# A two-layer graph kernel on one core: row sums of the neighbour lists on four column strips of TensorE, and two ScalarE steps in another order

## The chip, the core and the metric

One core of a Trainium2 chip runs the whole kernel. The metric is the device time of one execution in microseconds (us). Before the change three runs gave 2482.44, 2485.44 and 2485.81 us, so the median is 2485.44 us.

The engines are TensorE (PE; its weight loads are shown as PEld), VectorE (DVE), ScalarE (ACT), GpSimd (POOL) and SyncE (SP, which here only issues DMAs). Each works through its own queue in order, and they meet at semaphores.

## The reference

The input is a batch of 16 graphs with 1024 nodes and 64 features each, and an adjacency matrix of integers per graph, in which about 0.8% of the entries are set. Two layers follow each other, each with a residual and a layer norm:

```python
x = _layernorm(x + _L0_gnn_ref(x, adj, ...))   # eight heads
x = _layernorm(x + _L1_gnn_ref(x, adj, ...))   # one head
```

Layer 0 is attention in eight heads of 64 over the neighbours, with a bias per kind of edge and a leaky ReLU before the softmax:

```python
scores = einsum('bmhd,bnhd->bhmn', q, k) * scale + edge_bias
scores = leaky_relu(scores, 0.2); masked where edges == 0
out = einsum('bhmn,bnhd->bmhd', softmax(scores), v) @ Wp + bp
```

Layer 1 scores a pair by a leaky ReLU of a sum of two projections, weighed by a vector `a`:

```python
s = u[:, :, None, :] + v[:, None, :, :]
e = einsum('bijf,f->bij', where(s > 0, s, 0.2 * s), a); masked where adj == 0
h_prime = softmax(e) @ hp; return elu(h_prime)
```

## The kernel before, in words

Since few entries of the adjacency are set, the kernel works on lists of neighbours. Rows come in groups of eight (`GR`); a tile `t` holds 128 rows as 64 rows on each half of the partitions, and a batch has eight tiles (`NT`).

**The lists.** `prepare(b)` (from L318) is a generator that builds the lists of graph `b` in small pieces. For each half of the columns (`hs`) it loads eight tiles of the adjacency, turns each into bf16 zeros and ones in `ab` (L335), clears the diagonal on POOL (L340), and then adds up, for each group of eight rows and each column, a code in which every row of the group has its own bit. That is the sum over rows `pat` (L346): a matmul of `wz`, which holds the codes, with each of the eight `ab` tiles, 512 columns at a time. The 16 groups of tile `T` belong in the rows `16 T` to `16 T + 15` of `pat`. `wz` is mostly zero, and a window of 128 of its columns puts the block of codes where tile `T` needs it; all eight matmuls write all 128 rows of one PSUM bank and accumulate. DVE then reads `pat` into keys `ka` (L351) and picks the largest with max and match-replace (L357 to L392). At the end SP writes the lists to memory, from where they return as `cb`, spread over all partitions.

**One iteration.** The loop over `g` at the end of the kernel handles tile `g` of layer 0 and tile `u = g - 12` of layer 1. `at(layers, step, name)` issues one step of one tile, and the order of these calls is the order of each engine's queue: it was written out by hand, and nothing reorders it. `lists.place(g, k)` issues, at five places of an iteration, the pieces of list work that are due, and pieces of norm work. `t` is `g` modulo eight; some work comes only at certain `t`: the end of layer 1 of a graph at `t = 6`, the constants of the next graph at `t = 7`, the start of layer 1 at `t = 2` and its `sums` at `t = 3`.

The steps that matter here, in the order of an iteration:

- `score` (L642 on PE), which DVE reads into `sc` (L650); `gather` of layer 0 (L516 on PE, copied to `xg` on ACT, L522); `heads` (L710, odd tiles); `rows` into `back` (L289, L726); `queries` (L621, read on DVE into `qp`, L626).
- `residual` of both layers on DVE (L843, L732), which reads `back`.
- `project` of layer 1 (L777, L783): ACT and then DVE read `pz` into `r` (L789, L790).
- `gather` of layer 1, first half; then `turn_weights` of layer 1 (one transpose on PE, L818, and the copy `eT` on ACT, L820); then `turn` of layer 0 (eight transposes on PE, L535, and two copies `xn` on ACT, L536); then `gather` of layer 1, second half.
- `weigh` of layer 1 (L804 on PE: 12 matmuls in four strips of 32 columns into the bank `e`; DVE takes the row maximum `m`, L806), then `exps` of layer 1 (the exponential on ACT, L812, which needs `m`).
- `turn_weights` of layer 0 (L684 on PE into `pp`, two copies `w` on ACT, L686); `turn` of layer 1 (L535, L536).
- `own_rows` (the copy `rw` on ACT, L767, then `rq` on POOL, L769); `attend` of layer 0 (L694 on PE into `z`, which needs `w`; copied to `zT` on ACT, L699); `attend` of layer 1 (L829 on PE into `pa`, copied to `aT` on ACT, L834).

**Shared PSUM.** `back`, the transposed `eT` and the scores of `weigh` follow each other in one buffer (tag `e`): each must be read before the next is written. `z` and `pat` share another single buffer (tag `z`). The transposes `pt` of layer 0, `pp` and `pq` share two buffers (tag `p`), `pg`, `pa` and the transposes of layer 1 two more (tag `g`), and the scores `s`, `po` and `pz` two of tag `s`.

Of the kernel before, what the change touches and what calls it, by code (L numbers as in the profile page):

```python
# [12 lines left out]
ALU = mybir.AluOpType  # L13
# [16 lines left out]
BF16 = mybir.dt.bfloat16  # L30
# [3 lines left out]
def kernel(  # L34
# [4 lines left out]
    nc = tc.nc  # L39
    B, N, D = x.shape  # L40
    H = edge_bias.shape[1]
    HD = H * D
    P = 128
    NT = N // P
# [8 lines left out]
    fst = fast.enter_context(tc.tile_pool(name="fst", bufs=1))  # L53
# [15 lines left out]
    def sub(n):  # L69
        return slice(n * D, n * D + D)  # L70
# [42 lines left out]
    for h in range(H):  # L113
        c, r = h // 2, sub(h % 2)
# [89 lines left out]
    NGT = P // GR  # L204
# [10 lines left out]
    code_w = tmp.tile([P, 1], F32, name="code_w")  # L215
# [6 lines left out]
    in_g = fst.tile([P, NGT], F32, name="in_g")  # L222
# [4 lines left out]
    nc.vector.tensor_tensor(in_g, in_g, lt_g, ALU.mult)  # L227
    in_q = fst.tile([P, NQ], F32, name="in_q")
    nc.vector.tensor_tensor(in_q, in_g[:, 0:NQ], in_g[:, NQ : 2 * NQ], ALU.add)
    wz = fst.tile([P, 2 * P - NGT], BF16, name="wz")  # L230
    nc.vector.memset(wz, 0.0)
    nc.vector.tensor_scalar(wz[:, P - NGT : P], in_g, code_w, None, ALU.mult)
    rep_q = fst.tile([P, NQ, H, GR], BF16, name="rep_q")
    nc.vector.tensor_tensor(
        rep_q, in_q.unsqueeze(2).unsqueeze(3).to_broadcast([P, NQ, H, GR]),
# [82 lines left out]
    def prepare(b):  # L318
# [10 lines left out]
        for hs in range(2):  # L329
            ab = per.tile([P, NT, 2, SEG], BF16, tag="ab", name=f"ab_{b}_{hs}")  # L330
            for T in range(NT):
                ad = ads.pop(hs * NT + T)

                if b:
                    nc.vector.tensor_scalar(ab[:, T, :, :], ad, 1.0 - TINY, 0.0, ALU.subtract, ALU.max)  # L335
                else:
                    nc.scalar.activation(ab[:, T, :, :], ad, AF.Relu, bias=below)
                if T % 4 // 2 == hs:
                    own = ab[:, T, T // 4, ts(T % 2, P)]
                    nc.gpsimd.tensor_tensor(own, own, no_diag, ALU.mult)  # L340
                load(hs * NT + T + 4)
                if T % 2:
                    yield "sums" if T == NT - 1 else None
            pat = ps_z.tile([P, 2, SEG], F32, tag="z", name=f"pat_{b}_{hs}")
            for T in range(NT):
                nc.tensor.matmul(  # L346
                    pat.rearrange("p a c -> p (a c)"), wz[:, P - NGT - NGT * T : 2 * P - NGT - NGT * T],
                    ab[:, T, :, :].rearrange("p n (t r) -> p t n r", r=D), start=(T == 0), stop=(T == NT - 1),
                )
            yield "keys"  # L350
            nc.vector.scalar_tensor_tensor(  # L351
                ka[:, 2 * hs : 2 * hs + 2, 0:SEG], pat, float(KEY), revc.unsqueeze(1).to_broadcast([P, 2, SEG]),
                ALU.mult, ALU.add,
            )
            yield
            for s in range(2 * hs, 2 * hs + 2):
                nc.vector.max(lst[:, s, 0:8], ka[:, s, 0:SEG])  # L357
                nc.vector.match_replace(kb[:, s, 0:SEG], lst[:, s, 0:8], ka[:, s, 0:SEG], -1.0)
                yield
# [66 lines left out]
        for n in range(2):  # L426
            for q in range(NQ):
                r = slice(D * n + GR * q, D * n + GR * q + GR)
# [7 lines left out]
    def finish(b):  # L436

        flags, dg, rows_s = late.pop(b)
        mask = dbl.tile([P, NT, SLOTS], BF16, tag="mask", bufs=3, name=f"mask_{b}")
        nc.vector.tensor_scalar(mask[:, :, 0 : 2 * CAP2], rows_s, code, NEG, ALU.not_equal, ALU.mult)  # L440
        yield
        dgf = sml.tile([P, NT], F32, tag="dgf", bufs=2, name=f"dgf_{b}")
        nc.vector.tensor_scalar(dgf, dg, 1.0, None, ALU.is_ge)
        own = sml.tile([P, NT, GR], F32, tag="own", bufs=2, name=f"own_{b}")
        nc.vector.tensor_tensor(
            own, dgf.unsqueeze(2).to_broadcast([P, NT, GR]), own_i.unsqueeze(1).to_broadcast([P, NT, GR]), ALU.mult
        )
        nc.vector.tensor_scalar(mask[:, :, 2 * CAP2 : SLOTS], own, 0.0, NEG, ALU.is_equal, ALU.mult)
        yield
        nc.vector.tensor_scalar(dgf, dg, 2.0, None, ALU.is_ge)  # L450
        nc.vector.tensor_reduce(flags[:, 18:19], dgf, XX, ALU.max)
        fl = sml.tile([P, 1], F32, tag="fl", bufs=2, name=f"fl_{b}")
        nc.vector.tensor_reduce(fl, flags, XX, ALU.max)
        nc.vector.tensor_scalar(fl, fl, 0.5, None, ALU.is_ge)
        nc.vector.tensor_tensor(bad, bad, fl, ALU.max)
        masks[b] = mask
# [17 lines left out]
    class Tiles:  # L474


        def load(self, t):
            nm = f"{self.b}_{self.layer}_{t}"
            self.cb[t] = cb = dbl.tile([P, NSEG, 2, NQ, WIN], BF16, tag="cb", bufs=3, name=f"cb_{nm}")
            nc.sync.dma_start(  # L480
                cb.rearrange("p s n q k -> p (s n q k)"),
                edges[self.b][t].rearrange("s n q k -> (s n q k)").unsqueeze(0).to_broadcast([P, NSEG * 2 * NQ * WIN]),
            )
# [390 lines left out]
    l0, l1 = {}, {}  # L874

    def at(layers, step, name, *args):
        b, t = divmod(step, NT)
        if b in layers:
            getattr(layers[b], name)(t, *args)
# [28 lines left out]
    lists = Lists()  # L908
    with tc.manual_schedule(engines={getattr(mybir.EngineType, e) for e in order}):
        first = prepare(0)  # L910
        for _ in range(PIECES - 1):
            next(first)
        l0[0] = Layer0(0)
        for _ in lists.side.pop():
            pass
        l0[0].load(0)
        l0[0].load(1)
        l0[0].constants()
        for _ in first:
            pass  # L920
        l0[0].indicate(0)
        l0[0].own(0)
        for _ in finish(0):
            pass
        for g in range(NT * B + LAG + 7):
            u = g - LAG
            b, t = divmod(g, NT)
            if t == 0 and 0 < b < B:
                lists.side.insert(0, finish(b))
            lists.place(g, 0)  # L930
            at(l0, g - 2, "exps", 0, range(4))
            at(l0, g - 1, "score", lambda: at(l0, g - 2, "divide", 0))
            if (g - 1) // NT not in l0:
                at(l0, g - 2, "divide", 0)
            back = ps_z.tile([P, 3, D], F32, tag="e", name=f"back_{g}") if g > 3 else None
            at(l0, g - 2, "exps", 1, range(2))
            at(l0, g, "gather", 0)
            at(l0, g - 3, "heads")
            at(l0, g, "gather", 1)
            at(l0, g - 2, "exps", 1, range(2, 4))  # L940
            at(l1, u - 3, "rows", back)
            at(l0, g - 3, "rows", back)
            at(l0, g, "queries")
            if t == 6 and b - 2 in l1:
                lists.side.append(l1[b - 2].end())
            at(l1, u - 3, "residual")
            at(l0, g - 3, "residual")
            at(l0, g - 2, "divide", 1)
            at(l1, u - 1, "project")
            lists.place(g, 1)  # L950
            at(l1, u, "gather", 0)
            at(l1, u - 2, "turn_weights")
            at(l0, g - 1, "turn")
            lists.place(g, 2)
            at(l0, g + 1, "indicate")
            at(l0, g + 2, "load")
            at(l1, u, "gather", 1)
            at(l1, u - 1, "weigh")
            at(l1, u - 1, "exps")
            if t == 2 and b - 1 in l0:  # L960
                x1 = l0[b - 1].end()
            at(l0, g - 2, "turn_weights")
            at(l1, u - 1, "turn")
            lists.place(g, 3)
            at(l1, u + 1, "indicate")
            at(l1, u + 2, "load")
            at(l0, g + 1, "own")
            at(l1, u + 1, "own")
            at(l1, u, "own_rows")
            if t == NT - 1 and b + 1 < B:  # L970
                l0[b + 1].constants()
            at(l0, g - 2, "attend")
            at(l1, u - 2, "attend")
            lists.place(g, 4)
            if t == 2 and b - 1 in l0:
                l1[b - 1] = Layer1(b - 1, x1)
                del l0[b - 1]
                l1[b - 1].load(0)
            if t == 3 and b - 1 in l1:
                l1[b - 1].sums()  # L980
            if t == 4 and b + 1 < B:
                l0[b + 1] = Layer0(b + 1)
            if t == NT - AHEAD and b + 1 < B:
                l0[b + 1].load(0)
# [415 lines left out]
```

## Time and profile before

The profile is of one execution. Its own time was 2491.47 us, of which 2489.6 us are the span from the first to the last instruction.

| what | value |
|---|---|
| time of the profiled execution | 2491.47 us |
| its span | 2489.6 us |
| mean granted clock of TensorE | 0.969 |
| `pat` matmuls (L346), count and mean duration | 256, 390 ns |
| DVE keys `ka` waiting for `pat` | 114.2 us in 31 waits |
| layer 1's exponential (L812), count and mean duration | 128, 362 ns |
| copies `w` (L686), count and mean duration | 256, 588 ns |
| copies `xn` (L536), count and mean duration | 512, 601 ns |
| copies `eT` (L820), count and mean duration | 128, 269 ns |

A row of the groups' table gives the line, the engine, the operation and the tiles, then the busy time and the mean duration of one. Matmuls overlap, so the busy time of a group of them is less than count times duration. A line of the list of waits reads: engine, its tile and line, what it waited for, then the total in us, the number of waits and the longest. A wait is put down to the last releaser that the profile can see, which is not always the real one. In a timeline each line gives the start and the length in us, and in brackets the time for which the engine sat idle before it and who ended that.

Idle time of an engine which is not the one that sets the pace costs nothing; what a wait is worth must be read from the stretch in which it stands.

### The profile page before, as it was taken

To read this page: it belongs to the slowest core of one execution; us is meant where nothing else is said; L and a number is where in the kernel's file an instruction comes from. 1 tells how busy PE (TensorE), PEld (TensorE's weight loads), DVE (VectorE), ACT (ScalarE), POOL (GpSimd) and SP (SyncE) were. 2 spreads that over 40 slices of the span, in tenths; PEclk is the share of its full clock that TensorE was granted. 3 is DMA by queue.
4 is the path that set the end of the run, shared out by engine and by line. 5 is a ranking of instruction groups with operands and counts; after the bars stand their busy time and mean duration, and the time that the engine had idled before them with its cause. 6 is when DMAs were issued, how large, how long until landed. Compare 5 with 4: busy or idle time off the path is not lost. (4 is left out here: it accounts for less than half of the span.)

```text
span 2489.6 us, 107460 instructions
## 1 busy us (share of the span) xinstructions
PE 2260.9 (91%) x46658; PEld 1870.6 (75%) x46658; DVE 1813.8 (73%) x4591; ACT 1613.4 (65%) x5585; POOL 1206.3 (48%) x1570
## 2 busy tenths in 40 slices
PE   5577999999999999999999999999999999999995
PEld 3466878787787877778787777878777787888764
DVE  5688788687877868687787868778786877866432
ACT  2255666667676676766666676766766676677853
POOL 1133535545454554545455454545545454545552
PEclk8798999999999999999999999999999999999998
DMA  4422422423333242333324232332433233132111
GB/s 103 131 70 93 132 90 76 145 78 108 107 95 109 71 144 85 104 94 101 104 85 135 87 113 83 112 103 79 142 90 110 82 113 103 57 104 71 61 38 29
DMA packets 192691, 238.78 MB, mean 96 GB/s; under 512 B 91732, under 2 KB 157332, under 8 KB 192212
## 3 DMA queue, kind: packets, MB, share of 16 engines
q1 hardware_dynamic: 192212, 231.85, 30.1%
q8 instruction: 368, 6.03, 1.0%
q14 instruction: 111, 0.91, 0.1%
HBM read 226.58 MB, written 5.21 MB: 93 GB/s over the span
## 5 line engine op out<-in xcount | busy, mean ns | idle before, releaser
L516 PE MATMUL pg<-f,x 128*64 128x272 bf16 (+2 forms) x13312 | 811.7, 274 | 44.0 <-DVE f L492 29.0
L516 PEld LDWEIGHTS <-x 128*64 128x64 bf16 x13312 | 669.5, 110 | 154.0 <-issue 125.2
L676 POOL TENSOR_TENSOR ls<-ls,den 128x480 f32<-128x480 f32 x256 | 295.0, 1152 | 641.2 <-DVE den L675 640.1
L522 ACT COPY xg<-pg 128x448 f32<-128x448 f32 x512 | 268.0, 526 | 338.7 <-PE pg L516 338.1
L492 DVE TENSOR_SCALAR f<-cb,jrow 128x2176 bf16<-128x2176 bf16 x512 | 432.4, 885 | 15.0 <-DMA cb<-col_d 15.0
L668 ACT ACTIVATE ls<-ls,mx 128x120 f32<-128x120 f32 x1024 | 390.9, 385 | 0.0
L536 ACT COPY xn<-pt 120x512 f32<-120x512 f32 x512 | 277.9, 601 | 21.7 <-PE pt L535 21.6
L535 PE MATMUL pt<-ident,xg 128*120 128x128 f32 x2048 | 272.6, 275 | 19.6 <-DVE qp L626 17.2
L769 POOL TENSOR_TENSOR rq<-rw,in_q 128x960 bf16<-128x960 bf16 x128 | 229.9, 1796 | 114.8 <-ACT rw L767 114.8
L535 PEld LDWEIGHTS pt<-ident,xg 128*120 128x120 f32 x2048 | 230.7, 138 | 27.9 <-DVE qp L626 18.7
L650 DVE TENSOR_TENSOR sc<-s,rowc 128x480 f32<-128x480 f32 x256 | 156.0, 651 | 120.8 <-PE s L642 119.0
L694 PE MATMUL z<-w,xn 120*64 120x64 f32 x4096 | 173.2, 227 | 65.9 <-ACT w L686 65.8
L694 PEld LDWEIGHTS z<-w,xn 120*64 120x64 f32 x4096 | 146.6, 138 | 99.4 <-ACT w L686 93.9
L789 ACT ACTIVATE r<-pz 128x480 f32<-128x480 f32 x256 | 131.8, 567 | 123.1 <-PE pz L783 123.1
L790 DVE SCALAR_TENSOR_TENSOR r<-pz,r 128x480 f32<-128x480 f32 x256 | 155.6, 649 | 72.6 <-ACT r L789 72.3
L668 ACT ACTIVATION_READ_ACCUMULATOR ls<-ls,mx 128x1 f32 x1024 | 194.4, 190 | 0.0
L658 DVE SCALAR_TENSOR_TENSOR ls<-sc 128x480 f32<-128x480 f32 x256 | 181.3, 708 | 0.0
L659 DVE TENSOR_REDUCE mx<-ls 128x4 f32<-128x480 f32 x256 | 167.2, 653 | 8.8
L501 POOL COPY xg<-xT 128x64 f32<-128x64 f32 x256 | 104.0, 421 | 111.8 <-PE pt L535 111.8
L626 DVE TENSOR_TENSOR qp<-pq,qb 128x256 f32<-128x256 f32 x256 | 96.2, 417 | 76.8 <-PE pq L621 76.8
L642 PE MATMUL s<-xg,qp 64*64 64x120 f32 x4096 | 148.0, 286 | 4.1 <-DVE qp L626 3.4
L829 PE MATMUL pa<-eT,xn 120*64 120x8 f32 x4096 | 145.7, 202 | 4.8 <-ACT xn L536 3.9
(228 smaller groups left out, 4181.0 us busy)
## 6 DMA issues: line engine op xcount, KB each, us to landing
cb<-col_d SPq DMA_DIRECT2D x271, 544.0 KB
ad<-in_adj_dram SPq DMA_DIRECT2D x256, 256.0 KB
xs<-in_x_dram SPq DMA_DIRECT2D x32, 128.0 KB
rows_s<-slot_d SPq DMA_DIRECT2D x256, 14.0 KB
out_dram<-o SPq DMA_DIRECT2D x32, 128.0 KB
col_d<-col SPq DMA_DIRECT2D x128, 4.2 KB
dg<-in_adj_dram SPq DMA_DIRECT2D x32, 2.0 KB
slot_d<-slot SPq DMA_DIRECT2D x16, 28.0 KB
```

What stands on the lines that cost most here:

```text
L492: nc.vector.tensor_scalar(fj.rearrange("p s n q k -> p (s n q k)"), cb.rearrange("p s n q k -> p (s n q k)"), jrow[:, j : j + 1], None, AL ...
L516: nc.tensor.matmul(pg[sub(n), :, FIRST * a_ + lo : FIRST * a_ + to], self.t3[:, k, 4 * hs + 2 * a_ + j, :], f[j][:, 2 * hs + a_, n, :, lo:to],
L522: nc.scalar.copy(dst, pg)
L535: nc.tensor.transpose(pt[:, q, :], xg[:, 4 * m + q, :], ident)
L536: nc.scalar.copy(self.xn[t][:, ts(m, 4), :], pt)
L650: nc.vector.tensor_tensor(sc, both[n], self.rowc[:, n, ts_].unsqueeze(2).to_broadcast([P, 4, SLOTS]), ALU.add)
L658: nc.vector.scalar_tensor_tensor(ls, scs[n], SLOPE, scs[n], ALU.mult, ALU.max)
L659: nc.vector.tensor_reduce(self.mx[:, n, ts_], ls, XX, ALU.max, negate=True)
L668: nc.scalar.activation(ls[:, q, :], ls[:, q, :], AF.Exp, bias=neg[:, q : q + 1], accum_out=den[:, q : q + 1])
L676: nc.gpsimd.tensor_tensor(ls, ls, den.unsqueeze(2).to_broadcast([P, 4, SLOTS]), ALU.mult)
L694: nc.tensor.matmul(zz[sub(n), q, :], xn[:, q, sub(n)], w_[n][:, q // 2, sub(q % 2)], start=True, stop=True)
L769: nc.gpsimd.tensor_tensor(rq, rw.unsqueeze(1).to_broadcast([P, NQ, SLOTS]), in_q.unsqueeze(2).to_broadcast([P, NQ, SLOTS]), ALU.mult)
```

## The change

Three edits.

1. `wz` shrinks from 240 columns to 48: 16 zero columns, the 16 columns of codes, 16 zero columns.
2. The eight `pat` matmuls no longer write all 128 rows. Each writes 32 rows with a window of 32 columns of `wz`: tiles 0 and 1 write rows 0 to 31, tiles 2 and 3 rows 32 to 63, and so on. The even tiles come first and start their strip, then the odd tiles add to it and end it.
3. In an iteration, `turn` of layer 0 now stands before `turn_weights` of layer 1, and `exps` of layer 1 stands behind `turn_weights` of layer 0 and `turn` of layer 1. As these calls set the queues, the transposes L535 come before L818 on PE and the copies `xn` before `eT` on ACT; and the exponential L812 comes behind the copies `w` and `xn` on ACT. Nothing else moves: `weigh` and the maximum `m` stay, and so does every call to `lists.place`.

```diff
-    wz = fst.tile([P, 2 * P - NGT], BF16, name="wz")
+    wz = fst.tile([P, 3 * NGT], BF16, name="wz")
     nc.vector.memset(wz, 0.0)
-    nc.vector.tensor_scalar(wz[:, P - NGT : P], in_g, code_w, None, ALU.mult)
+    nc.vector.tensor_scalar(wz[:, NGT : 2 * NGT], in_g, code_w, None, ALU.mult)
...
-            for T in range(NT):
+
+            for T in (*range(0, NT, 2), *range(1, NT, 2)):
                 nc.tensor.matmul(
-                    pat.rearrange("p a c -> p (a c)"), wz[:, P - NGT - NGT * T : 2 * P - NGT - NGT * T],
-                    ab[:, T, :, :].rearrange("p n (t r) -> p t n r", r=D), start=(T == 0), stop=(T == NT - 1),
+                    pat[16 * (T - T % 2) : 16 * (T - T % 2) + 32, :, :].rearrange("p a c -> p (a c)"),
+                    wz[:, NGT - NGT * (T % 2) : NGT - NGT * (T % 2) + 32],
+                    ab[:, T, :, :].rearrange("p n (t r) -> p t n r", r=D), start=(T % 2 == 0), stop=(T % 2 == 1),
                 )
...
             at(l1, u, "gather", 0)
+            at(l0, g - 1, "turn")
             at(l1, u - 2, "turn_weights")
-            at(l0, g - 1, "turn")
             lists.place(g, 2)
             at(l0, g + 1, "indicate")
             at(l0, g + 2, "load")
             at(l1, u, "gather", 1)
             at(l1, u - 1, "weigh")
-            at(l1, u - 1, "exps")
             if t == 2 and b - 1 in l0:
                 x1 = l0[b - 1].end()
             at(l0, g - 2, "turn_weights")
             at(l1, u - 1, "turn")
+            at(l1, u - 1, "exps")
             lists.place(g, 3)
```

## The prediction

> **What bounds the kernel now.** First the page's busy shares, then busy time by stretches. I cut the steady part at the first score matmul of layer 1 (`weigh`, L804), one stretch for each of eight iterations, and name a stretch by the `t` of the iteration whose `weigh` opens it. The columns are stretch, length, busy PE, PEld, DVE, ACT, POOL, granted clock, DMA share, GB/s. In order they are t = 6, 7, 0, 1, 2, 3, 4, 5.
>
> ```profile
> PE 2260.9 (91%) x46658; PEld 1870.6 (75%) x46658; DVE 1813.8 (73%) x4591; ACT 1613.4 (65%) x5585; POOL 1206.3 (48%) x1570
> 1018.54:1036.76 18.22, 15.51 (x320) 13.01 (x318) 11.34 (x26) 13.82 (x52) 12.49 (x18) 1.00 0.49 160
> 1036.76:1057.27 20.51, 19.70 (x432) 15.53 (x430) 13.10 (x35) 14.29 (x58) 9.70 (x16) 1.00 0.38 135
> 1057.27:1075.51 18.24, 16.89 (x320) 14.19 (x318) 14.73 (x35) 11.60 (x41) 11.59 (x17) 0.91 0.46 136
> 1075.51:1093.88 18.37, 18.37 (x368) 14.62 (x366) 11.83 (x35) 12.57 (x44) 5.06 (x7) 1.00 0.18 63
> 1093.88:1112.12 18.24, 16.29 (x351) 13.77 (x349) 17.48 (x52) 11.46 (x35) 7.92 (x11) 1.00 0.18 65
> 1112.12:1132.67 20.55, 19.20 (x392) 16.33 (x390) 16.93 (x41) 12.56 (x44) 10.14 (x13) 0.92 0.44 121
> 1132.67:1149.62 16.95, 16.95 (x383) 14.69 (x381) 14.32 (x31) 11.93 (x36) 12.37 (x14) 1.00 0.19 69
> 1149.62:1166.07 16.45, 16.45 (x359) 13.83 (x358) 12.73 (x34) 11.60 (x40) 6.79 (x9) 1.00 0.23 49
> ```
>
> The reader sees that PE never rests in t = 1, 4 and 5: there, a microsecond off PE is a microsecond off the time. PE idles in t = 6, 0, 2, 3. In t = 2 DVE is busy 17.48 of 18.24: what PE gains there DVE may take back. In t = 0 and 3 the mean clock is below 1. Next the list of waits, for what PE idles on.
>
> ```profile
> PE z L694 <- ACT w L686: 65.8, 123, 1.5
> ACT e L812 <- DVE m L806: 112.3, 100, 2.4
> PE pt L818 <- DVE den L675: 19.5, 26, 1.2
> ```
>
> The first two belong together, as the timeline of t = 2 shows (start, length, engine, line):
>
> ```profile
> 1095.40 1.04 PE L535 MATMUL pt<-ident,xg 128*120 128x128 f32 x8
> 1096.63 0.27 DVE L806 TENSOR_REDUCE m<-e 128x1 f32<-128x120 f32 x1
> 1096.94 0.36 ACT L812 ACTIVATE e<-e,m 128x120 f32<-128x120 f32 x1 [2.42 <-DVE m L806]
> 1097.29 1.06 ACT L686 COPY w<-pp 120x512 f32<-120x512 f32 x2
> 1097.92 0.33 PE L694 MATMUL z<-w,xn 120*64 120x64 f32 x2 [1.48 <-ACT w L686]
> ```
>
> The maximum `m` is late because DVE has list work first. ACT waits 2.42 us for it with the copies `w` queued behind the exponential, and PE waits 1.48 us for `w`, whose inputs were there all along. By stretch, over the eleven batches of eight stretches from 579 to 2187 us, the z wait is 0.33 us in t = 6, 1.35 in t = 0, 1.64 in t = 2, 1.25 in t = 3, none elsewhere. Its companion is the clock:
>
> ```profile
> 1065.00:1067.00 2.00, 2.00 (x37) 1.58 (x28) 1.36 (x5) 1.20 (x7) 2.00 (x4) 0.50 0.81 234
> ```
>
> Read in 1 us stretches, the clock falls to half for some 3.4 us 13 times in these batches, each costing 1.7 us: five in t = 0, one in t = 2, seven in t = 3, all 5 to 6 us after `weigh`, just behind a z wait; never in the other stretches.
>
> Last, the sums and what speaks for four strips:
>
> ```profile
> 933.82 1.90 PE L346 MATMUL pat<-ab,wz 128*128 128x512 bf16 x8
> 935.64 1.05 PE L642 MATMUL s<-xg,qp 64*64 64x120 f32 x32
> ...
> 1002.15 0.62 PE L804 MATMUL e<-r,a_two 128*32 128x120 f32 x16
> 1002.59 0.24 PE L804 MATMUL e<-mask,ident_b 128*32 128x120 bf16 x4
> ...
> 1018.22 0.27 ACT L820 COPY eT<-pt 120x128 f32<-120x128 f32 x1
> 1018.54 0.36 PEld L804 LDWEIGHTS e<-r,a_two 128*32 128x32 f32 x16 [0.24 <-ACT eT L820]
> ```
>
> Eight sums take 1.82 us to the next group; at 379 ns each and 1.90 in all they start 0.217 us apart, one after another. `weigh` already uses four strips of 32 columns: its four bf16 matmuls of 216 ns each all lie within 0.24 us. The last two lines are t = 6, where `weigh` waits for the copy `eT`.
>
> [...] no run shows four strips at 512. [...] Here a 128x32 bf16 load takes 97 ns against 98 for the 128x128, so I charge nothing for it. [...]
>
> **The change part by part.** All sums are against the profiled execution, 2491.47 us (span 2489.6 and 1.9 around it); the median of the runs is 2485.44, so I subtract 6.0 at the end.
>
> *Sums.* Four strips side by side, two rounds: 2 x 0.217 = 0.43[...] (the bf16 group of `weigh` needs 0.17 to the next start with one short round), 0.59 against 1.82: 1.23 saved. Of 32 groups 26 lie from 310 us on, in t = 7 and 1: 32 us. The six before wait for POOL, ACT and DVE (9.4, 2.2 and 2.0 us in all); I take 2 us. What is late next in t = 1 is `zT`, whose release the sums need (same PSUM ring). Without the exponential in front, ACT must wait for the first transposes `pp`, some 0.3 us more than now, so `zT` ends 0.15 us too late there: 13 x 0.15 = -2. DVE idles 3 to 4 us before it reads the sums, so it follows. Sum: 32. Bounds: 0 if the strips run in turn, 41 if all 32 groups gain 1.27. The setup edit (a smaller `wz`) is one memset behind the weight preparation: nothing.
>
> *Late exponential.* `w` now follows `pp` directly, and z can start when L535 ends. The exponential then waits for `m` behind the copies `xn`, about 3.4 us after `weigh`; `m` comes at 3.0 at worst, and its result is needed only in the next iteration. Behind it on ACT are `rw` (for POOL) and `zT`, needed late except for the sums. For t = 0 I followed the stretch from 1788 us: with PE 1.2 us earlier the DVE times stay, but `pz` still finds `sc`, the transposes find `qp` and `weigh` finds `r` (margins 0.5, 0.2 and 0.9 us). All 1.35 us count: 13 batches, 17.6. In t = 2 they do not: `sc` ends at 1105.64, fixed by DVE, and `pz` starts at 1106.08, so only 0.4 is gained. In t = 3 the u sum on DVE comes earlier by its own wait of 1.25 us, then `po` waits for `sc`; I find `po` near 1121.25 instead of about 1122.2 (1123.57 less one clock drop), so 0.95 for t = 2 and 3 together: 12.4. Sum 30; bounds 8 (DVE takes all but t = 0 in part) and 58 (no DVE limit).
>
> *Clock.* 13 drops in 11 batches, 26 us over 13 batches. If z no longer waits they have no cause; but new waits of 1.1 us or so appear before `pz`, `po` and, in t = 6, `weigh`. The waits of 1.17 and 1.20 us in t = 6 beside gathers never brought a drop. I take half, 13; bounds -10 and 26.
>
> *Order of the turns.* L535 goes before L818, and so two `xn` copies (1.09 us) before `eT` on ACT. Gain: L818 waits for DVE's read of `back` (same PSUM ring), 1.18 us in t = 6 and 0.29 in t = 2; now L535 fills that. Loss: `weigh` needs `eT` gone. In seven stretches the second `xn` copy ends 0.77 us before `weigh`, so `eT` behind it leaves about 0.6. In t = 6 it ends 0.93 after: `weigh` starts 1.0 late, and everything behind it (`pp`, z, `m`), while POOL's norm chain, which sets the middle of that stretch, shifts by about 0.2. So I let t = 6 lose 0.2 net: -3; bounds -24 (the full 1.0 and a clock drop every second time) and +6.
>
> The sum: 32 + 30 + 13 - 3 = 72. 2491.5 - 72 = 2419.5; as a median 2413.5, rounded to 2413.
>
> **The rivals.**
> - DVE takes the place of the z wait: nothing from the exponential in t = 2 and 3, half in t = 0, and the clock no better: 32 + 9 - 3 = 38, 2447. For: 17.48 of 18.24. Against: t = 0 and 3 hold DVE waits for PE.
> - DVE does not bind and all drops go: 32 + 58 + 26 + 6 = 122, 2363. Against: `sc` in t = 2.
> - The strips run in turn, so that the change doesn't do what it says: 0 + 30 + 13 - 3 = 40, 2445. Against: `weigh`.
> - Slower: `eT`, last of three ACT copies, gates `weigh` in every stretch, not in one of eight. My margin is 0.6 us; if the copy comes later than that by 0.56 us in each of 128 stretches, the 72 us are gone, and from there it decides. At 0.7 us, 90 us lost: 2503. Against: ACT idles 0.26 to 0.88 us before the next copy `xg` in those stretches.
>
> **How the numbers follow.** Forecast 0.56; DVE 0.17; everything 0.14; strips in turn 0.05; slower 0.08. The forecast's own range is 2398 to 2430. The range of 8 in 10 takes in the two cases at 2445 and 2447 and half of the third: 2378 to 2450. A change of under 0.2% (5 us) can't be told from none. Faster 0.89, same 0.03, slower 0.08.
>
> **What would show it.** L346: eight matmuls in about 0.6 us. L694 without waits for `w`; L812 without stalling `w`. No half clock behind z in t = 0 and 3. New: PE waiting before L777 in t = 2 and L710 in t = 3, `weigh` waiting for `eT` in t = 6. L804 waiting for `eT` everywhere, or drops in t = 6, would make it wrong.

## The result, and the profile after

The changed kernel takes 2476.05 us (median of 20 runs, 2469.09 to 2485.86), the kernel before on the same chip 2487.56 us (20 runs, 2479.69 to 2500.03). The ratio is 0.9948, 95% interval 0.9936 to 0.9959: about 0.5% faster, some 12 us where 72 were forecast, and outside the forecast's range. The profiled execution has a span of 2474.2 us and a mean clock of 0.964, below the 0.969 of before.

First the page's busy shares, then the same eight stretches as before (t = 6, 7, 0, 1, 2, 3, 4, 5, cut at `weigh`; length, busy PE, PEld, DVE, ACT, POOL, granted clock, DMA share, GB/s):

```profile
PE 2230.1 (90%) x46658; PEld 1852.8 (75%) x46658; DVE 1858.2 (75%) x4591; ACT 1602.8 (65%) x5585; POOL 1227.3 (50%) x1570
```

```profile
1007.87:1024.33 16.46, 15.32 (x317) 12.86 (x318) 12.09 (x25) 12.66 (x50) 11.50 (x16) 1.00 0.52 173
1024.33:1044.80 20.47, 18.34 (x432) 14.87 (x430) 14.10 (x36) 14.25 (x58) 10.56 (x17) 1.00 0.39 136
1044.80:1060.40 15.60, 15.60 (x319) 13.04 (x317) 14.37 (x34) 11.56 (x42) 10.29 (x15) 1.00 0.51 158
1060.40:1077.54 17.14, 17.14 (x367) 14.04 (x365) 13.11 (x36) 12.49 (x44) 6.73 (x9) 1.00 0.22 68
1077.54:1095.21 17.67, 16.66 (x351) 14.04 (x350) 16.95 (x50) 11.28 (x35) 7.34 (x10) 1.00 0.19 67
1095.21:1117.31 22.10, 19.12 (x392) 15.88 (x390) 18.93 (x44) 12.50 (x44) 11.77 (x14) 0.92 0.39 112
1117.31:1134.11 16.80, 16.80 (x384) 14.59 (x382) 14.33 (x31) 11.85 (x36) 12.37 (x14) 1.00 0.19 70
1134.11:1151.38 17.27, 16.35 (x360) 13.72 (x358) 12.71 (x34) 12.50 (x43) 6.95 (x9) 1.00 0.19 48
```

Two things stand out. The instruction counts are the same, yet DVE is busy 44 us longer (1858.2 against 1813.8). And t = 0 and 1 are shorter with PE at work throughout, while t = 3 is longer than before (22.10 against 20.55), with DVE busy 18.93 us instead of 16.93. The means over the eleven steady batches say the same, in us, with some of the kernels tried below:

| stretch | 6 | 7 | 0 | 1 | 2 | 3 | 4 | 5 | sum |
|---|---|---|---|---|---|---|---|---|---|
| before | 18.21 | 20.16 | 17.71 | 18.36 | 18.37 | 19.94 | 16.96 | 16.44 | 146.15 |
| after | 16.46 | 21.13 | 15.65 | 17.14 | 17.67 | 22.77 | 16.80 | 17.26 | 144.88 |
| `strips_only` | 18.22 | 20.75 | 16.79 | 17.12 | 19.07 | 19.04 | 16.94 | 16.43 | 144.36 |
| `rq_late` | 16.46 | 21.43 | 15.66 | 17.11 | 17.79 | 19.76 | 16.80 | 17.26 | 142.27 |
| `rqlate_const5` | 16.46 | 19.66 | 15.70 | 17.11 | 17.79 | 19.47 | 16.80 | 18.48 | 141.47 |
| `best_quota` | 16.53 | 18.22 | 16.41 | 17.08 | 17.54 | 18.43 | 16.80 | 18.38 | 139.39 |

From before to after, t = 6, 0, 1 and 2 gain 1.75, 2.06, 1.22 and 0.70 us a batch; t = 3 gives back 2.83, t = 7 0.97 and t = 5 0.82. (The wait for `eT` ahead of t = 6's `weigh` is counted in t = 5.)

The list of waits shows what PE idles on now:

```profile
PE po L712 <- DVE sc L652: 45.3, 14, 4.7
PE pz L779 <- DVE sc L652: 13.9, 15, 1.0
PE e L806 <- ACT eT L822: 13.2, 15, 0.9
PE z L696 <- ACT w L688: 5.6, 16, 1.2
```

The wait of z for `w` is gone as forecast, 65.8 down to 5.6. The wait of `po` for `sc` was 6.8 us in all and is 45.3: most of what the exponential gave has turned into it. It stands in t = 3. Here is the timeline of that stretch (start, length, engine, line; in brackets the idle time before, and who ended it):

```profile
1099.03 0.38 ACT L769 ACTIVATE rw<-mask,ones 128x120 bf16<-128x120 bf16 x1
1099.47 3.01 DVE L494 TENSOR_SCALAR f<-cb,jrow 128x2176 bf16<-128x2176 bf16 x2
1099.49 2.40 POOL L771 TENSOR_TENSOR rq<-rw,in_q 128x960 bf16<-128x960 bf16 x1 [0.77 <-ACT rw L769]
...
1105.71 1.21 DVE L652 TENSOR_TENSOR sc<-s,rowc 128x480 f32<-128x480 f32 x2
1106.41 1.06 PE L712 MATMUL po<-zT,wvp 64*64 64x128 f32 x6 [2.98 <-DVE sc L652]
```

And the same place before:

```profile
1115.69 1.47 DVE L492 TENSOR_SCALAR f<-cb,jrow 128x2176 bf16<-128x2176 bf16 x2
1117.15 0.43 ACT L767 ACTIVATE rw<-mask,ones 128x120 bf16<-128x120 bf16 x1
1117.66 1.79 POOL L769 TENSOR_TENSOR rq<-rw,in_q 128x960 bf16<-128x960 bf16 x1 [2.67 <-ACT rw L767]
```

Before, `rw` came after the pair of `f`, since ACT had stood waiting 2.13 us for the maximum `m`, with the exponential, `w`, `xn` and `rw` following each other in its queue (they start at 1114.90, 1115.25, 1116.19 and 1117.15). Freed of that wait, ACT issues `rw` before the pair, and POOL's `rq` starts 0.02 us behind DVE's first `f`. Now both take longer: the pair 3.01 us instead of 1.47, `rq` 2.40 instead of 1.79. The maxima and `sc` behind the pair in DVE's queue are late by as much, and PE waits 2.98 us for `sc`. The view in 2 us stretches shows the price behind the wait (the seventh value is the clock):

```profile
1104.00:1106.00 2.00, 0.00 (x0) 0.00 (x0) 1.97 (x6) 0.01 (x1) 0.61 (x1) 1.00 0.67 197
1106.00:1108.00 2.00, 1.59 (x22) 1.31 (x26) 1.97 (x5) 0.00 (x0) 0.91 (x1) 0.56 0.89 264
1108.00:1110.00 2.00, 2.00 (x32) 1.53 (x26) 1.56 (x3) 0.63 (x2) 0.40 (x1) 0.59 0.80 276
```

PE does nothing from 1104 to 1106, and its clock halves just after. In the eleven batches this comes in every t = 3; PE time lost to the half clock there is 2.17 us a batch (1.09 before), while the 0.78 us of t = 0 are gone.

The sums themselves did what the edit says, as the timeline of t = 7 shows:

```profile
1031.11 0.62 PE L347 MATMUL pat<-ab,wz 128*32 128x512 bf16 x8
1031.65 0.82 PEld L644 LDWEIGHTS s<-xg,qp 64*64 64x64 f32 x32 [0.42 <-issue]
...
1032.84 1.35 PE L518 MATMUL pg<-f,x 128*64 128x272 bf16 x22
1035.35 0.42 PE L518 MATMUL pg<-f,x 128*64 128x272 bf16 x4 [1.15 <-issue]
```

Eight matmuls now take 0.54 us to the start of the next group, against 1.82. But some 2.5 us into what follows PE stops for 1.15 us in the middle of a run of equal matmuls with no releaser in the profile ("issue"). Such waits come to 0.32 us a batch in t = 7 before and 1.45 after. Together with a wait of 0.98 us for the copy `xg` (0.20 before) they eat the gain there.

### The profile page after: what moved, and what is told of

Read it like the earlier page. It is cut to its first block, busy times and chain, and to the rows that moved or that the text cites. A ratio compares the mean times of both kernels' runs of the same rounds, so it can differ in the third digit from the quotient of the medians.

```text
span 2474.2 us, 107346 instructions
## 1 busy us (share of the span) xinstructions
PE 2230.1 (90%) x46658; PEld 1852.8 (75%) x46658; DVE 1858.2 (75%) x4591; ACT 1602.8 (65%) x5585; POOL 1227.3 (50%) x1570
## 5 line engine op out<-in xcount | busy, mean ns | idle before, releaser
L518 PE MATMUL pg<-f,x 128*64 128x272 bf16 (+2 forms) x13312 | 822.5, 276 | 43.5 <-DVE f L494 28.7
L494 DVE TENSOR_SCALAR f<-cb,jrow 128x2176 bf16<-128x2176 bf16 x512 | 457.9, 935 | 11.4 <-DMA cb<-col_d 11.4
L537 PEld LDWEIGHTS pt<-ident,xg 128*120 128x120 f32 x2048 | 224.2, 138 | 66.3 <-DVE qp L628 33.5
L771 POOL TENSOR_TENSOR rq<-rw,in_q 128x960 bf16<-128x960 bf16 x128 | 235.8, 1842 | 69.7 <-ACT rw L769 69.6
L688 ACT COPY w<-pp 120x512 f32<-120x512 f32 x256 | 138.1, 590 | 63.2 <-PE pp L686 63.2
L696 PE MATMUL z<-w,xn 120*64 120x64 f32 x4096 | 155.4, 229 | 5.6 <-ACT w L688 5.6
L503 POOL COPY xg<-xT 128x64 f32<-128x64 f32 x256 | 110.9, 450 | 93.1 <-PE pt L537 93.0
L696 PEld LDWEIGHTS z<-w,xn 120*64 120x64 f32 x4096 | 135.9, 141 | 28.2 <-ACT w L688 27.5
L779 PE MATMUL pz<-xg,w2d 64*64 64x480 f32 x1024 | 143.0, 571 | 13.9 <-DVE sc L652 13.9
```

Source lines behind the costliest of these rows:

```text
L494: nc.vector.tensor_scalar(fj.rearrange("p s n q k -> p (s n q k)"), cb.rearrange("p s n q k -> p (s n q k)"), jrow[:, j : j + 1], None, AL ...
L518: nc.tensor.matmul(pg[sub(n), :, FIRST * a_ + lo : FIRST * a_ + to], self.t3[:, k, 4 * hs + 2 * a_ + j, :], f[j][:, 2 * hs + a_, n, :, lo:to],
L537: nc.tensor.transpose(pt[:, q, :], xg[:, 4 * m + q, :], ident)
L696: nc.tensor.matmul(zz[sub(n), q, :], xn[:, q, sub(n)], w_[n][:, q // 2, sub(q % 2)], start=True, stop=True)
L771: nc.gpsimd.tensor_tensor(rq, rw.unsqueeze(1).to_broadcast([P, NQ, SLOTS]), in_q.unsqueeze(2).to_broadcast([P, NQ, SLOTS]), ALU.mult)
L779: nc.tensor.matmul(pz[n][sub(c_), :, :], w2d[sub(n), :], xg[sub(n), :, :].rearrange("p (g c) k -> p c g k", c=2)[:, c_, :, :], start=True, ...
```

## The experiments

The theory was that POOL's `rq`, moved into DVE's `f`, sets t = 3. The rivals were that one of the two order edits is bad by itself, that the sums don't pay, and that DVE has too much list work in t = 2 and 3 whatever POOL does. In the diffs, lines are against the kernel named.

**The parts of the change alone.** `strips_only` undoes both order edits in the changed kernel, `order_only` makes them alone in the kernel before.

```diff
-            at(l0, g - 1, "turn")
             at(l1, u - 2, "turn_weights")
+            at(l0, g - 1, "turn")
...
             at(l1, u - 1, "weigh")
+            at(l1, u - 1, "exps")
...
             at(l1, u - 1, "turn")
-            at(l1, u - 1, "exps")
```

> Only the sums on four strips; both order edits are undone. Theory A (the order edits cost in the stretch t = 3 what they gain elsewhere: POOL's rq now runs at the same time as DVE's f, f's busy time there rises from 5.1 to 7.0 us and po waits 3 us for sc): the strips alone keep their 1.28 us in each of the 26 groups of the steady part, about 30 us, ratio to before near 0.988, and PE shows no wait before po in t = 3. Theory B (the strips' gain itself is lost in t = 7 and 1, to ACT and POOL): ratio 0.993 to 0.997.

Measured: 2463.47 us, ratio 0.9913 (0.9884 to 0.9942). The sums alone give 22 us, more than the whole change, though less than the 0.988 that was expected of them. They gain 1.24 us a batch in t = 1; in t = 7 they lose 0.59, with 1.68 us of waits without a releaser. In t = 3 of the eleven batches PE has no wait for `sc`.

For `order_only` the same lines, the other way round, in the kernel before.

> Only the two order edits, sums as before. Theory A: slower than before by about 16 us, ratio 1.006, with the same wait of some 3 us before po in t = 3 and a half clock there in every batch. Theory B: the order edits gain some 10 us by themselves, ratio 0.996 or less.

Measured: 2488.77 us, ratio 1.0011 (0.9999 to 1.0023): nothing that can be told from no change, and so between the two expectations. Its stretches explain how: t = 6 and 0 win 1.74 and 1.96 us a batch, and t = 3 loses 2.45. The half clock comes in nine of the eleven t = 3, not in every one.

```profile
PE po L710 <- DVE sc L650: 43.4, 14, 4.7
```

The wait of `po` is the same as in the whole change, so it comes from the order edits, not from the sums.

`strips_late` undoes only the swap of the two turns in the changed kernel.

```diff
-            at(l0, g - 1, "turn")
             at(l1, u - 2, "turn_weights")
+            at(l0, g - 1, "turn")
```

> The whole change but for the swap of the two turns (turn_weights of layer 1 stays ahead of turn of layer 0). Theory A: the wait of weigh for eT at t = 6 (0.92 us a batch) goes and L818's wait (1.2 us) comes back, so within 5 us of the change, ratio to before 0.993 to 0.997; t = 3 stays as bad. Theory C (the swap is what costs): 15 us or more below the change, ratio 0.989 or less.

Measured: 2470.05 us, 0.9935 (0.9909 to 0.9960); the change with the swap has 0.9948. The swap is worth nothing that these runs can see in the whole time. In t = 3 `po` still waits 2.27 us a batch for `sc`, so the wait comes with the late exponential.

**Moving `rq` away from `f`.** `rq_late` is the changed kernel with one call moved, so that `rw` and `rq` come behind both attends:

```diff
-            at(l1, u, "own_rows")
...
             at(l0, g - 2, "attend")
             at(l1, u - 2, "attend")
+            at(l1, u, "own_rows")
```

> The whole change, with own_rows of layer 1 (ACT's rw and with it POOL's rq) moved behind both attends, so that rq starts about 1.2 us later. Theory A: f's busy time in t = 3 goes back to about 5.1 us, the wait before po from 3.1 to about 1.5 us or less and the half clock there comes less often; some 25 us below the change, ratio to before near 0.985. Theory D (DVE's own list work in t = 2 and 3 is what binds, POOL has no part in it): f's time falls but po still waits 2.5 us or more, ratio 0.993 to 0.997.

Measured: 2448.9 us, 0.9848 (0.9823 to 0.9874), 1% better than the change. Of the 2.6 us a batch, t = 3 gives 3.0 (22.77 to 19.76). Its timeline:

```profile
1086.13 1.47 DVE L494 TENSOR_SCALAR f<-cb,jrow 128x2176 bf16<-128x2176 bf16 x2
1086.56 0.40 ACT L769 ACTIVATE rw<-mask,ones 128x120 bf16<-128x120 bf16 x1
1087.04 2.21 POOL L771 TENSOR_TENSOR rq<-rw,in_q 128x960 bf16<-128x960 bf16 x1 [1.66 <-ACT rw L769]
1090.84 1.21 DVE L652 TENSOR_TENSOR sc<-s,rowc 128x480 f32<-128x480 f32 x2
1091.54 1.66 PE L712 MATMUL po<-zT,wvp 64*64 64x128 f32 x32 [1.44 <-DVE sc L652]
```

The pair of `f` is back at 1.47 us: 1.54 less than 3.01. PE's wait for `sc` is 1.44: 1.54 less than 2.98. The loss to the half clock in t = 3 falls from 2.17 to 0.47 us a batch. Here `rq` starts 0.91 us after the pair's start, inside the second `f`, and it is `rq` that grows (2.21 us), not the pair.

One caution: DVE's whole time for `f` hardly moves (457.9 to 456.7 us), since `rq` now starts 0.69 us behind the start of a pair in t = 2 (3.06 us, with `rq` at its 1.79). What it no longer meets there is an integer instruction of the lists, `left` (L380), which had taken 1.7 us beside `rq` and 0.19 otherwise. All of DVE's busy time falls by 8.9 us only (1858.2 to 1849.3): most of the gain is in which stretch pays.

**Bringing the same collision into the kernel before.** `rq_early_before` is the kernel before with `own_rows` moved up behind `weigh`, and nothing else.

```diff
             at(l1, u - 1, "weigh")
+            at(l1, u, "own_rows")
...
-            at(l1, u, "own_rows")
...
             at(l0, g - 2, "attend")
```

> The kernel before with one move: own_rows of layer 1 directly behind weigh, so that ACT makes rw while it waits for m, and POOL's rq starts some 3 us earlier, where DVE runs layer 0's f. Theory A (a POOL tensor operation beside f slows f): f's busy time over a batch of eight stretches rises from 27.1 us to 30 or more, and where DVE is full (t = 2) the wait before pz appears; ratio to before 1.002 to 1.010, though ACT has less to do behind m. Theory A wrong (f doesn't mind POOL): f's time stays at 27 us and the kernel is the same or faster.

Measured: 2540.38 us beside 2492.58, ratio 1.0186 (1.0161 to 1.0212), more than was expected. The group of `f` before, and in this kernel (busy time and mean of one in ns, then DVE's idle time ahead of it):

```profile
L492 DVE TENSOR_SCALAR f<-cb,jrow 128x2176 bf16<-128x2176 bf16 x512 | 432.4, 885 | 15.0 <-DMA cb<-col_d 15.0
```

```profile
L492 DVE TENSOR_SCALAR f<-cb,jrow 128x2176 bf16<-128x2176 bf16 x512 | 505.9, 1029 | 11.8 <-DMA cb<-col_d 11.8
```

The same 512 instructions take 73.5 us more, and nothing was moved but `rw` and `rq`. In t = 2 z then waits 3.2 us a batch for `w`, and the clock halves behind it in every batch, which makes the loss larger than the collisions alone.

Counted over the whole trace, by the POOL instruction that overlaps a pair of `f` most (`rqlate_noswap` comes below):

| kernel | pairs beside `rq` | of these over 2.5 us | their mean |
|---|---|---|---|
| before | 13 | 0 | 1.48 us |
| `strips_only` | 13 | 0 | 1.48 us |
| `order_only` | 15 | 13 | 2.80 us |
| `strips_late` | 14 | 13 | 2.90 us |
| after | 14 | 13 | 3.02 us |
| `rq_late` | 26 | 13 | 2.26 us |
| `rqlate_noswap` | 13 | 0 | 1.47 us |
| `rq_early_before` | 51 | 50 | 3.23 us |

Pairs beside no POOL work take 1.47 to 1.48 us in all of them. With `own_rows` in its old place the long pairs come with the late exponential, with or without the swap and the sums, and not without it. In the kernel before the pairs touch `rq` for less than 0.1 us, at its edge.

In the changed kernel, 14 pairs at 1.55 us more make 21.7 of the 25.5 us by which the group of `f` grew (432.4 to 457.9). The other large part of DVE's extra time is the casts `ab` of the adjacency (L335), 98.9 us before and 125.5 after, longer in the same way: 12 pairs took 2.06 us beside POOL's last addition of layer 1 (L860), and pairs beside most other POOL work some 0.75. They lie in t = 6, where PE doesn't wait for them, and `rq_late` leaves them (121.4). The maxima and match-replaces of the lists take 0.40 to 0.45 us beside any POOL work and beside none.

The timelines show how the delay falls on the two, and no run shows what makes one hold the other up. Of the 13 long pairs in the changed kernel nine are like the one above: the first `f` takes 0.78 us, as by itself, `rq` is 0.61 us longer than 1.79 and ends at 1101.89, and the second `f` ends 0.59 us after that, 2.31 us long. In the other four the first `f` takes 2.40 us and the second 1.13, and `rq` keeps its 1.79. In all 13 `rq` starts 0.02 to 0.03 us behind the first `f`, so its start doesn't tell which of the two comes. In `rq_late` it does: `rq` starting 0.69 us behind the pair's start (t = 2), still beside the first `f`, doubles the pair, and `rq` starting 0.91 us behind it (t = 3), inside the second `f`, is itself the longer. So a shift of less than a microsecond on ACT decides who pays.

**The waits without a releaser in t = 7.** The constants of the next graph stand there: 64 matmuls with their weight loads on PE (L608) and two steps on DVE. The waits end 9 to 13 us after `weigh`, inside or just behind stretches in which all DMA engines are busy:

```profile
1029.00:1031.00 2.00, 2.00 (x76) 1.95 (x68) 0.41 (x2) 1.97 (x9) 0.86 (x4) 1.00 1.03 324
1031.00:1033.00 2.00, 2.00 (x66) 1.47 (x64) 1.18 (x2) 1.85 (x12) 2.00 (x3) 1.00 1.00 385
1034.00:1035.40 1.40, 0.25 (x6) 0.08 (x4) 1.36 (x4) 0.29 (x2) 1.37 (x2) 1.00 0.09 31
```

(The eighth value is the DMA share: 1.03, 1.00, then 0.09 while PE stands.) The page also lists two DMA queues of the kind "instruction". This is the larger (packets, MB, share of the 16 engines' span), the same before, after and in `rqlate_const5`; the page doesn't say for which engine it is:

```profile
q8 instruction: 368, 6.03, 1.0%
```

The idea to try, a guess of the author's, was that PE runs out of instructions during a burst of transfers, all the sooner if it has just used up many short ones. `rqlate_const5` is `rq_late` with the constants two iterations earlier.

```diff
-            if t == NT - 1 and b + 1 < B:
+            if t == NT - 3 and b + 1 < B:
                 l0[b + 1].constants()
```

> rq_late with the constants of the next graph (64 matmuls L608 and their weight loads on PE, and two DVE steps) issued at t = 5 in place of t = 7. Theory F (behind the strips PE runs out of instructions at t = 7[...], and the constants just ahead use many): the PE waits without a releaser at t = 7, 1.3 us a batch in rq_late, fall below 0.4, and the time by some 12 us, ratio near 0.980. Theory G (those waits come from something else at t = 7, and only move): ratio 0.983 to 0.987.

Measured: 2439.58 us, 0.9800 (0.9778 to 0.9823), by the ratios some 12 us better than `rq_late`. In t = 7 the waits without a releaser fall from 1.35 us a batch to 0.34 and the stretch from 21.43 to 19.66, while t = 5, where the constants now are, grows by 1.22. The burst itself stays where it was: from 6 to 10 us after `weigh` in t = 7 the DMA share is 0.99 in `rq_late` and 1.01 here. What moved are instructions of PE and DVE. So the edit shows that these instructions, where they stood, brought most of the waits, and not that the burst did. That PE lacks instructions there would fit, but isn't shown, since no view shows when an instruction arrives; nor did a run move the burst.

**Is the swap worth something once `rq` is out of the way?** `rqlate_noswap` is `rq_late` with the diff of `strips_late`.

```diff
-            at(l0, g - 1, "turn")
             at(l1, u - 2, "turn_weights")
+            at(l0, g - 1, "turn")
```

> rq_late with the two turns in the order of before. By the stretches of the change against strips_late the swap gained 0.8 us over t = 5 and 6 and 0.7 each at t = 0 and 2, and lost 0.75 at t = 7 and, at t = 3, what DVE took back. With DVE freed at t = 3 the swap should gain: this run 8 to 18 us above rq_late, ratio 0.988 to 0.992. If the swap is worth nothing: 0.984 to 0.986.

Measured: 2452.43 us, 0.9851 (0.9828 to 0.9874), beside 0.9848 with the swap. A miss: the swap makes t = 6, 0 and 2 together 3.15 us a batch shorter, but t = 3, 5 and 7 give 2.78 back. The question isn't answered cleanly, since `rq` is not out of the way with the swap (13 long pairs, in t = 2) and is without it (none; the group of `f` takes 432.5 us, as before the change).

**Without the late exponential, does moving `rq` still help?** `strips_rq_late` is `strips_only` with the move of `rq_late`.

```diff
-            at(l1, u, "own_rows")
...
             at(l0, g - 2, "attend")
             at(l1, u - 2, "attend")
+            at(l1, u, "own_rows")
```

> The strips alone (exponential and turns as before the change), with own_rows moved behind both attends as in rq_late. Theory A (rq meets f only because the order edits make rw, and so rq, earlier): here f in t = 3 is 4.1 us already, so the move gains nothing, within 6 us of strips_only, ratio to before 0.989 to 0.994. Theory E (the move is worth 25 us in any order, so rq_late says nothing about the change): ratio 0.983 or less.

Measured: 2461.59 us, 0.9884 (0.9862 to 0.9905), against 0.9913 (0.9884 to 0.9942) without the move; the intervals overlap. So the move pays 1.0% with the order edits and about 0.3% without them, which can't be told from nothing. That fits: in `strips_only` `rq` lengthens no pair, so there is no such collision to remove.

**The share of list work.** `rqlate_quota` spreads the list pieces of `rq_late` over the stretches in another way.

```diff
-    QUOTA = (3, 3, 5, 6, 6, 6, 6, 6)
+    QUOTA = (4, 5, 6, 6, 5, 4, 5, 6)
```

> rq_late with the list work spread otherwise over the eight iterations (same 41 pieces a graph, less at t = 2, 3 and 4, more at t = 6, 7 and 0). Theory D2 (what is left of the waits before pz at t = 2 and po at t = 3, 1.1 and 1.4 us a batch, is DVE's list work): both fall below 0.5 and the time by 15 us or more, ratio near 0.979. Otherwise the work is missed or blocks in the new places: ratio 0.985 or more.

Measured: 2477.91 us, 0.9956 (0.9944 to 0.9969), a clear miss. The sums moved into t = 0, where PE waits 3.1 us a batch for `zT` with the clock halved behind it (2.02 us). A milder shift, `best_quota`, on top of `rqlate_const5`:

```diff
-    QUOTA = (3, 3, 5, 6, 6, 6, 6, 6)
+    QUOTA = (4, 3, 5, 6, 5, 5, 6, 7)
```

> rqlate_const5 with one piece of list work each moved from t = 2 and t = 3 to t = 6 (of the iteration before) and t = 5; the sums stay at t = 7 and t = 1. A piece is about 1 us of DVE. If DVE's work at t = 2 and 3 is what is left (waits before pz 1.1 and po 1.4 us a batch), these two waits fall by about 1 us each: 12 to 25 us below rqlate_const5, ratio near 0.973. If something else holds pz and po: 0.979 to 0.982.

Measured: 2418.37 us beside 2492.58, ratio 0.9706 (0.9680 to 0.9732): the fastest version, faster than both kernels. No pair of `f` is lengthened by `rq` in it (13 were in `rqlate_const5`), so not all of its gain need come from the list work.

```profile
PE po L712 <- DVE sc L652: 12.0, 14, 4.7
PE e L806 <- ACT eT L822: 13.0, 15, 0.9
```

The wait of `po` is down from 45.3 us to 12.0, and no half clock is left in t = 3.

Two variants on top. `best_rq_mid` is `rqlate_const5` with `own_rows` put behind `project` instead:

```diff
             at(l1, u - 1, "project")
+            at(l1, u, "own_rows")
...
             at(l1, u - 2, "attend")
-            at(l1, u, "own_rows")
```

> rqlate_const5 with own_rows of layer 1 issued in the middle of the iteration, behind project, where DVE runs list work and r and not f. Theory A: f over a batch falls below 26 us and the waits before pz and po shrink: 5 to 15 us below rqlate_const5, ratio 0.974 to 0.978. Against it: rw delays the copy xg on ACT at t = 6, which is already late there; then 0.980 or more.

Measured: 2466.39 us, 0.9900 (0.9872 to 0.9927), a miss: `rw` then holds up the copies `xg` and `eT` on ACT, and `weigh` waits 2.3 us a batch for `eT`.

`best_noorder` is `best_quota` with both order edits undone (the diff of `strips_only`).

```diff
-            at(l0, g - 1, "turn")
             at(l1, u - 2, "turn_weights")
+            at(l0, g - 1, "turn")
...
             at(l1, u - 1, "weigh")
+            at(l1, u - 1, "exps")
...
             at(l1, u - 1, "turn")
-            at(l1, u - 1, "exps")
```

> best_quota with both order edits of the change undone (exponential directly behind weigh, turns as before). If the late exponential is worth what the prediction said once DVE has room at t = 2 and 3, z waits for w again at t = 0, 2 and 3 (some 3 us a batch, with half clocks behind them): 30 to 60 us above best_quota, ratio to before 0.982 to 0.995. If the order edits are worth nothing in themselves: within 8 us of best_quota, ratio 0.968 to 0.974.

Measured: 2447.13 us beside 2491.41, 0.9813 (0.9788 to 0.9837). The order edits, worth nothing in the kernel before, are worth 1.1% here (0.9813 against 0.9706), some 27 us, just under the 30 to 60 expected.

## Why the prediction was wrong, step by step

The forecast was 2413 (2378 to 2450), and 2476 came: the direction was right, most of the gain wasn't there. On the eleven steady batches the account closes.

- *Sums.* The strips run side by side, and the size was right: 1.28 us a group against 1.23, and t = 1 gained 1.22. (Of the 0.59 us forecast for a group, 0.43 are the two rounds and 0.16 the author's estimate, from the 0.17 to the next start at `weigh`.) Wrong in t = 7, where the step took the microsecond off PE as a microsecond off the time. With the sums alone (`strips_only`) waits without a releaser take 1.36 us a batch more there and the half clock 0.47, and the stretch is 0.59 longer. With the swap the transposes wait 0.98 us for `xg` (0.20 in `strips_late`, which lacks it). In the whole change the stretch is 0.97 longer instead of 1.23 shorter: 2.2 us in each of 13 batches, 29 us.
- *Late exponential, t = 0.* The number came, but partly by luck: 1.35 plus the half clock of 0.78 make 2.13, and 2.06 came. Yet `strips_only` has 0.92 of it, half clock included, with z still waiting 1.17 us there. The late exponential adds 0.27 to that (`strips_late`, 16.52), since PE then waits 0.66 us for DVE ahead of `turn_weights` of layer 1 (L820); the swap, which the prediction booked at nothing in t = 0, adds 0.87.
- *Late exponential, t = 2 and 3.* This is the step that failed: "I find `po` near 1121.25 instead of about 1122.2 (1123.57 less one clock drop), so 0.95 for t = 2 and 3 together". It slid PE and the u sum, and held the other durations on DVE fixed. But an ACT that no longer waits sends `rw` earlier; `rq` follows, and DVE's `f` doubles beside it. The two stretches grew by 2.13 us instead of shrinking by 0.95 and half their clock loss, 0.63: 3.7 us a batch, 48 us in 13. The prediction named `rw` as "needed late", looking at who needs it and not at whom it disturbs. The trace before had the sign: 28 pairs of `f` took 2.46 us beside POOL's `less_x` (L468), and 13 integer `left` (L376) 1.66 us beside `rq` instead of 0.19.

  Even without the collision in t = 3 the 0.95 isn't there. In `rq_late` the two stretches less their clock loss take 37.08 us, in `rqlate_noswap`, where `rq` lengthens no pair at all, 37.01, before 37.06. Batches without a half clock alone give 37.1 for `rq_late` and 37.4 before. So the rival "DVE takes the place of the z wait: nothing from the exponential in t = 2 and 3" was close to right there.
- *Clock.* Forecast 13 us gained; instead the loss moved, from t = 0 to t = 3, where "new waits of 1.1 us or so" turned out 3.0 us long. Of the waits named, those of `pz` (1.01 us in t = 2) and `weigh` (0.92) brought no drop. That waits cause the drops was the author's estimate, from where they stand; that those of t = 0 ended with the z wait isn't shown, since `strips_only` has none there either. A drop also costs less than the 1.7 us taken: in t = 3 before, stretches with one last 20.53 us and most of those without 19.16, so 1.37. And each of the 13 drops before is 3.41 us long, while the idle time ahead of it in t = 0 is only two waits of 1.19 and 0.16 us. (The drops begin 5.9 to 6.4 us after `weigh`, a little later than it says.)
- *Order of the turns.* The wait for `eT` is 0.92 us a batch where 1.0 was forecast. The stretches t = 5 and 6 together gained 0.93 instead of losing 0.2, but the runs without the swap show no gain in the end, near the -3 us.

The misses of t = 7 and of t = 2 and 3, 29 and 48 us, less 15 won in t = 5 and 6 and about 8 in the others, are 54 us. The profiled execution was to take 2419.5 us and took 2476.1: 56.6.

Of the rivals, the one at 2447 had the right engine for two stretches but not the cause that did most of the harm. That `eT` gates every `weigh`, the slower case, didn't happen: PE waits 13.2 us for it in all.

What stays open: what PE lacks in the waits of t = 7, and why behind a wait of one length the clock halves in some batches and not in others.

## What to carry to other kernels

When an edit frees an in-order queue, everything behind the freed place moves earlier, also what nobody is waiting for: follow each such instruction to the engine it starts, and look at what runs beside it then. An instruction that is "needed late" can still run beside another engine's at the wrong moment and lengthen it (here the pair of `f`, from 1.47 us to 3.01), so look in the trace for instructions of one shape with two durations, and see what another engine did during the long ones. A saved wait is worth something only where the next engine has room: here the same two edits were worth nothing or 1.1%, depending on where `rq`, the constants and the list pieces stood.

## What the runs showed of the hardware

- A POOL tensor-tensor of 128x960 beside two DVE `tensor_scalar` of 128x2176 bf16 takes 2.40 us instead of 1.79, and the two 3.01 instead of 1.47, in nine of 13 cases after the change; in the other four it keeps its 1.79 and the two take 3.44. The profile books this as busy time of both, not as a wait, so no list of waits shows it.
- An integer tensor-tensor of 128x32 took 1.74 us beside the same POOL instruction and 0.19 beside none; max and match-replace stayed at 0.40 to 0.45.
- Four strips of 32 columns with 512 columns of data run side by side: eight matmuls in 0.54 us instead of 1.82, 3.4 times.
- Behind longer waits of PE the clock halved more often, without a sharp limit. Ahead of `po` in t = 3, waits of 1.44 us had this behind them in 3 of 11 batches (`rq_late`) and 1 of 11 (`rqlate_const5`), of 2.27 in 8 (`strips_late`), of 2.98 in 9 (`order_only`), of 2.98 to 3.43 in all 11 (after); waits of 0.9 and 1.0 us at `weigh` and `pz` after in none. Length alone doesn't decide: 1.55 us ahead of `po` in t = 1 of `rqlate_quota` had no half clock behind them in 11 batches, z waits of 1.19 us in t = 0 before the change in 5.
